# A graph layer on one Trainium2 core: six more message buffers, 128-column first halves, and another spread of the last groups' products

## Chip, cores and metric

The kernel runs on one core of one Trainium2 chip. The metric is device time in microseconds of one execution, shown as the median of several runs. A profile is one further execution, taken by the hardware profiler; its span goes from the first to the last instruction.

## The reference

A pre-normalised relational graph layer on 12,500 nodes of 256 features with 212,500 edges, sorted by destination, each of one of 8 types. There are 200,000 random edges (both directions of 100,000 pairs) and a self edge for every node.

```
h    = relu(layernorm(x))                        # 12500 x 256
hx   = einsum('ni,rio->rno', h, weight)          # 8 x 12500 x 256
msg  = hx[edge_type, src]                        # 212500 x 256
agg  = segment_sum(msg, dst, 12500)
out  = x + agg * 0.5**0.5 + bias + (h @ loop_weight) * 0.5**0.5
```

## The kernel before

It sums first and multiplies afterwards: for each destination node and each type it sums the rows of h, and then multiplies the sums by that type's weight.

**Edges.** The sorted edges lie in units: one partition of an index block holds one unit of 267 consecutive edges (256 in the first block). Self edges of a unit (up to 22) are taken out and added in another way, so that 256 slots, two tiles of 128, hold the rest. Whether all edges were covered is counted, and a general path (line 120) would run behind the rest if not; it does not run here. There are 802 units and 1603 tiles. For a tile, `gather` (line 742) fetches 128 rows of 1 KB into a message tile with one indirect DMA from GpSimd's queue. The rows come from the normalised table h, which the kernel itself writes at the start; before it is complete they come from x and are normalised on chip in batches of four tiles (`batch`, line 1136, and `moments`, line 699). Tile t + AHEAD is gathered in iteration t of the main loop (line 1159). Message tiles are allocated in pairs, MSGS / 2 = 30 pairs; a gather waits until the pair that had its buffer 60 tiles earlier has been multiplied. From the second block on, every tile whose number is 47 modulo 48 is fetched with 128 row DMAs of SP (`load_sources`, line 762) instead, up to t + AHEAD < 1603.

**Sums.** `onehots` (line 779) makes, for four tiles in one VectorE instruction, a matrix with a one where an edge's node and type stand: 176 columns, that is 22 nodes by 8 types from the unit's base node. It is called in every fourth iteration for the tiles from t + LEAD + 2 on, in 2 + LEAD / 4 buffers. `edge_sums` (line 806) multiplies the message tile's two halves of 128 features with it, into one of four PSUM banks per unit. The unit's second multiplied tile holds its first 128 edges; its product covers only `REACH[0][1]` = 13 nodes, 104 columns, except in the last block (tiles from 1536 on), where both cover 22 nodes, 176 columns. In the profile each matmul call is two instructions, so a tile has four. `add_sums` (line 831) adds a unit's bank, one unit behind, to the sums `acc` in SBUF, at an offset from a register; `acc` is a ring of six groups of 128 nodes.

**Groups.** The 12,500 nodes are 98 groups of 128 (the last has 84). `Plan` bounds, from straight lines with a margin, which nodes a unit can touch: `low` and `high`. `plan.last[g]` is the last unit that can touch group g, and after its `add_sums` the group is ready: 18 products (`product`, line 1003, two instructions each: two for h times the loop weight from `self_t`, sixteen for the sums) are put into `queue` with a time from which they may go (`ready`, DELAY = 6 tiles later, less at the end) and one by which they must (`until`). Lines 1207 to 1214 take out as many products per tile as the queue's `until` values demand, after the tile's own matmuls. The products of group g go to the bank `outs[g % 2]`, whose second half holds the bias. After the last one, `last` puts `finish` (line 1021) into a list, to be run REST = 3 tiles later: it adds the bias and the bank to the rows of x and stores them. What is left when the loop ends runs after it (line 1239), lists before products.

**Row buffers.** Tiles of 4 x 128 rows (`rowp`, six buffers) carry, in order of allocation, the 26 pieces of x that are normalised and written to h, and then the rows of x and h that the groups need. When the last piece is normalised (`norms_end`, line 1123, in iteration 28), SP loads bias and weights (`load_weights`, line 1105); six iterations later VectorE copies the bias into the banks and ScalarE scales the weights (`scale_weights`, line 1114).

**Order.** Each engine executes its instructions in the order in which the loop issues them; only waits on semaphores connect engines. GpSimd's queue holds the gathers, SP's all other DMAs. The column tiles (`cols`, three buffers) hold the one-hot positions of a block of 256 tiles; `marks` holds the marks and the diagonal matrix with which `find_types` (line 910) finds, once every four groups, the types of the self edges.

Of the kernel before, what the change touches and what calls it, by code (L numbers as in the profile page):

```python
# [9 lines left out]
F32 = mybir.dt.float32  # L10
BF16 = mybir.dt.bfloat16
# [11 lines left out]
P = 128  # L23
# [4 lines left out]
XG = 4  # L28


EDGES = 267
# [1 line left out]


WIN = 22
REACH = ((0, 13), (0, 22))

GROUP = 128

# [1 line left out]
CLEARED = 3  # L41
RING = GROUP * SLOTS

MSGS = 60
AHEAD = 58

SINGLE = 48
FETCH = 4
# [2 lines left out]


QUAD = 4
LEAD = 8
PAIR = 2
LAG = 1
BANKS = 4
# [1 line left out]

DELAY = 6  # L60
REST = 3

BATCH = 4

# [15 lines left out]
class Plan:  # L80
# [7 lines left out]
    def __init__(self, N, E):  # L88
        U = PAIR * P
        first = P * U  # L90
        self.NU = NU = -(-E // U) if E <= first else P + -(-(E - first) // EDGES)
        self.EU = E - (NU - 1) * U if E <= first else E - first - (NU - P - 1) * EDGES
        self.NT = NU * PAIR - (1 if self.EU <= P else 0)
        self.rate = N / E * EDGES
        s = 6.5 * (E / 4) ** 0.5 + EDGES

        lines = [(U, 0), (EDGES, first - P * EDGES)]
        last = (1.1 * EDGES, 1.1 * (first - P * EDGES) - 0.1 * E - 1.5 * EDGES + s)
        self.low = [(a * N / E, (b - s) * N / E) for a, b in [*lines, last]]
        self.high = [(a * N / E, (b + s) * N / E) for a, b in lines]  # L100
        self.starts = list(range(0, N, GROUP))
        self.ends = self.starts[1:] + [N]
        self.NG = len(self.starts)
        self.last = [
            min([NU - 1, *(int((e + 2 - b) / a) + 1 for a, b in self.low)]) for e in self.ends]
        self.last[-1] = NU - 1
        self.first = [
            max(0, min(int((s - WIN - 2 - b) / a) for a, b in self.high) - 1) if s else 0
            for s in self.starts]

        self.blocks = [
            [k for k in range(1, -(-NU // P))
             if max(a * P * k + b for a, b in self.low) <= e + 2
             and max(a * min(NU - 1, P * k + P - 1) + b for a, b in self.high) + WIN + LASTS + 2 >= s]
            for s, e in zip(self.starts[::XG], self.starts[XG::XG] + [N])]
        self.typed = min([q for q, b in enumerate(self.blocks) if b], default=len(self.blocks))
        assert XG * self.typed >= SLOTS
# [102 lines left out]
def kernel(  # L220
# [11 lines left out]
    nc = tc.nc  # L232
    N, D = x.shape
    E = src.shape[0]
    R = weight.shape[0]
    KC = D // P
    C = R * max(n for _, n in REACH)
    assert KC * R * WIN <= 512
    plan = Plan(N, E)
# [17 lines left out]
    const = ctx.enter_context(tc.tile_pool(name="const", bufs=1))  # L257
    ident = const.tile([P, P], F32, name="ident")
    eps = const.tile([P, 1], F32, name="eps")
    ones = const.tile([P, 1], F32, name="ones")  # L260
    bias_in = const.tile([P, D], F32, name="bias_in")
    w = const.tile([P, KC, R * D], F32, name="w")
    wl = const.tile([P, KC, D], F32, name="wl")
    low = const.tile([P, NB], F32, name="low")
# [17 lines left out]
    with ExitStack() as main:  # L282
# [4 lines left out]
        ep = main.enter_context(tc.tile_pool(name="ep", bufs=1))  # L287
        rowp = main.enter_context(tc.tile_pool(name="rowp", bufs=ROWS))
        idx = main.enter_context(tc.tile_pool(name="idx", bufs=2))
        cols = main.enter_context(tc.tile_pool(name="cols", bufs=3))  # L290
        small = main.enter_context(tc.tile_pool(name="small", bufs=4))
        msgs = main.enter_context(tc.tile_pool(name="msgs", bufs=MSGS // PAIR))
        ohs = main.enter_context(tc.tile_pool(name="ohs", bufs=2 + LEAD // QUAD))
# [2 lines left out]
        marks = main.enter_context(tc.tile_pool(name="marks", bufs=1))  # L296
# [16 lines left out]
        firsts, stops, loops, marked, typed, gidx, col = {}, {}, {}, {}, {}, {}, {}  # L313
# [168 lines left out]
        def columns(b, got):  # L482


            halves = [(slice(i * P, (i + 1) * P), o, n)
                      for i, (o, n) in enumerate(REACH if b < NB - 1 else ((0, WIN), (0, WIN)))]

# [422 lines left out]
        def find_types(q):  # L910

            ptt = pt[:, : XG * (LASTS + 2)].rearrange("p (g k) -> p g k", g=XG)

            def find():
                parts = [(b, m, i) for b, m in marked.pop(q) for i in range(2)]
                for g in range(XG):
                    for b, m, i in parts:
                        nc.tensor.matmul(
                            ptt[:, g, :], m[:, i, g * GROUP : (g + 1) * GROUP], loops[b][:, i, :],
                            start=(b, m, i) == parts[0], stop=(b, m, i) == parts[-1])  # L920

            def kinds_of():
                place_ = small.tile([P, XG], F32, name="place_")
                nc.vector.tensor_scalar(
                    place_, ptt[:, :, LASTS], float(-plan.starts[XG * q]), None, op0=ALU.add)
                nc.vector.tensor_tensor(place_, place_, ptt[:, :, LASTS + 1], op=ALU.add)
                nc.vector.tensor_tensor(place_, node, place_, op=ALU.subtract)
                one = small.tile([P, XG, LASTS], F32, name="one")
                nc.vector.tensor_tensor(
                    one, line[:, :LASTS].unsqueeze(1).to_broadcast([P, XG, LASTS]),  # L930
                    place_.unsqueeze(2).to_broadcast([P, XG, LASTS]), op=ALU.is_equal)
                nc.vector.tensor_tensor(one, one, ptt[:, :, :LASTS], op=ALU.mult)
                kinds = small.tile([P, XG], F32, name="kinds")
                nc.vector.tensor_reduce(kinds, one, AX.X, ALU.add)  # L934
                marked[q] = marks.tile([P, XG * GROUP], BF16, name="diagonal")
                for g in range(XG):
                    nc.scalar.activation(  # L937
                        marked[q][:, g * GROUP : (g + 1) * GROUP], ident, AF.Copy,
                        scale=kinds[:, g : g + 1])

            shared(find, [(2, kinds_of)])

            def spread():
                nc.tensor.matmul(pt, ones_b, marked.pop(q), start=True, stop=True)

            def types_of():
                typed[q] = types.tile([P, XG * GROUP], BF16, name="types")
                nc.scalar.activation(typed[q], pt, AF.Copy)

            shared(spread, [(1, types_of)], lambda: q in marked, wait=2)  # L950

        got = {}
# [104 lines left out]
        with tc.manual_schedule():  # L1057
# [19 lines left out]
            for f in load[1 : 1 + head]:  # L1077
                f()
            for t in range(min(AHEAD, NT)):
                gather(t)  # L1080
# [22 lines left out]
                           for g in range(CLEARED, min(SLOTS, plan.NG))]  # L1103

            def load_weights():
                nc.sync.dma_start(
                    bias_in, bass.AP(tensor=bias.tensor, offset=bias.offset, ap=[[0, P], [1, D]]))
                for c in range(KC):
                    nc.sync.dma_start(
                        w[:, c, :].rearrange("p (r o) -> p r o", r=R),  # L1110
                        weight[:, c * P : (c + 1) * P, :].rearrange("r p o -> p r o"))
                    nc.sync.dma_start(wl[:, c, :], loop_weight[c * P : (c + 1) * P, :])

            def scale_weights():
                for o in outs:
                    i = nc.vector.tensor_copy(o[:, 1, :], bias_in)
                done["bias"] = i.ins.name
                for c in range(KC):
                    nc.scalar.mul(w[:, c, :], w[:, c, :], scale)
                    nc.scalar.mul(wl[:, c, :], wl[:, c, :], loop_scale)  # L1120
                done["weights"] = True
# [37 lines left out]
            for t in range(NT):  # L1159
# [57 lines left out]
                while waiting and (len(waiting) > LAG or t == NT - 1):  # L1217
                    u, ps = waiting.pop(0)
                    add_sums(u, ps)
                    while (next_group < plan.NG and plan.last[next_group] <= u  # L1220
                           and (done["weights"] or (NT <= 400 and done["norm"] == len(pieces)))):
                        g = next_group
                        while background and NT <= 400:
                            step()
                        until = PAIR * (plan.first[g + SLOTS] - 3) - REST if g + SLOTS < plan.NG else NT - 1
                        ready = t + max(0, min(DELAY, NT - 1 - t - 2 * DELAY))
                        until = max(ready, min(until, ready + int(GROUP / plan.rate * PAIR)))
                        if g and g % SLOTS == 0:
                            wrap(g)
                        work = [] if g else group_ahead(0)  # L1230
                        work += group_work(g)
                        if g + 1 < plan.NG:
                            work[-8:-8] = group_ahead(g + 1)
                        for c, f in work:
                            queue.append((ready, until, c, f))
                        next_group += 1
# [36 lines left out]
```

## Time and profile before

| | us |
|---|---|
| median of 3 runs | 2020.34 |
| the runs | 2019.54, 2020.34, 2027.53 |
| profiled execution | 2021.12 |
| its span | 2019.4 |
| PE busy, matmul instructions | 1776.1, 10411 |
| PE's busy time in `edge_sums`, in `product` | 1127.6; 901.5 + 107.8 |
| GpSimd busy | 1497.1 |
| VectorE busy | 1318.5 |
| ScalarE busy | 218.5 |

The granted TensorE clock averages 0.951 of full speed; in the windows it is 0.50 from 50 to 100 us, 0.60 from 100 to 150, and 0.93 to 1.00 after that. Times of an engine in the profile are those of its own instructions; a DMA that GpSimd issues counts there with the time that the issue takes, and the transfer runs on. Matmuls overlap, so that the mean duration of one is longer than the distance between two starts. In groups of instructions the columns are line, engine, operation, what is written and read, count, busy us, mean ns of one, and the idle time before them with what ended it; a releaser is inferred, and where the engine named had long been done it was another. "L758" is the gather's line, L821 the matmul of `edge_sums`, L835 the add of `add_sums`, L1012 the matmul of `product`, L1024 and L1025 the adds of `finish`, L788 the one-hots, L716 the normalising, L736 the write of h.

### The profile page before, as it was taken

What the parts mean: (1) busy time and instruction counts of PE and PEld (TensorE: products, weight loads), DVE (VectorE), ACT (ScalarE), POOL (GpSimd) and SP (SyncE); (2) the same over time, 40 slices, a digit from 0 to 9 for tenths busy, and PEclk for the clock granted to TensorE, in tenths of its full rate; (3) what the DMA queues carried; (4) which work ended last, traced back from release to release, by engine and by line L of the source; (5) the groups of instructions that cost most, each with busy time, mean ns of one, the idle gap of its engine ahead of it and who ended that gap; (6) DMA issues with size and microseconds to landing.
All of it is one profiled execution on the core that took longest, in us unless ns stands there. A gap on an engine that the chain in (4) does not pass through costs nothing.

```text
span 2019.4 us, 36387 instructions
## 1 busy us (share of the span) xinstructions
PE 1776.1 (88%) x10411; PEld 1585.9 (79%) x10411; DVE 1318.5 (65%) x3282; ACT 218.5 (11%) x470; POOL 1497.1 (74%) x1602
## 2 busy tenths in 40 slices
PE   2458999998998898999998998898998898988998
PEld 2357999997888888888777777787787787877886
DVE  7869667687665578656577655578565568665642
ACT  7844110000000000000000000000000000000000
POOL 7757777777777777777777777777777777777773
PEclk8569999998999999999999999999999999999999
DMA  8963443444444444444444444444444444444442
GB/s 296 378 219 100 148 137 106 128 144 122 128 140 120 139 137 119 128 118 139 130 126 139 128 125 134 129 127 140 128 118 139 127 122 129 119 139 122 118 121 70
DMA packets 152577, 281.63 MB, mean 139 GB/s; under 512 B 31149, under 2 KB 101940, under 8 KB 152372
## 3 DMA queue, kind: packets, MB, share of 16 engines
q0 software_dynamic: 75648, 206.67, 34.6%
q1 hardware_dynamic: 76724, 72.61, 11.3%
q8 instruction: 82, 1.34, 0.3%
q14 instruction: 123, 1.01, 0.2%
HBM read 253.55 MB, written 25.60 MB: 138 GB/s over the span
## 4 chain that ended last, share of the span: by engine, by line
PE 36%; DMA 19%; SPq 15%; issue 13%; POOL 8%; DVE 5%; ACT 2%; DVEq 0%; ACTq 0%; POOLq 0%
PE ps L821 19%; PE po L1012 17%; DMA msg<-h,gidx 14%; SPq L770 11%; POOL msg L758 8%; SPq L765 3%; ACT xt L716 1%; DMA h<-xt 1%; DMA hr<-h 1%; DMA msg<-h 1%; DVE e_stats L704 1%; DVE acc L835 1%; DMA w<-in_L_gnn_weight_dram 1%; DVE oh L788 1%; DMA xr<-in_x_dram 1%
## 5 line engine op out<-in xcount | busy, mean ns | idle before, releaser
L758 POOL DMA_INDIRECT msg<-h,gidx x1480 | 1404.0, 949 | 464.9 <-issue 365.4
L821 PE MATMUL ps<-oh,msg 128*128 128x176 f32 (+1 forms) x6412 | 1127.6, 305 | 219.3 <-DMA msg<-h,gidx 88.3
L821 PEld LDWEIGHTS ps<-oh,msg 128*128 128x128 f32 x6412 | 1023.4, 197 | 377.5 <-DMA msg<-h,gidx 175.6
L1012 PE MATMUL po<-w,acc 128*128 128x256 f32 x3136 | 901.5, 390 | 0.7 <-DVE acc L835 0.7
L835 DVE TENSOR_TENSOR acc<-acc,ps 128x352 f32 x802 | 415.4, 518 | 496.2 <-PE ps L821 490.0
L1012 PEld LDWEIGHTS po<-w,acc 128*128 128x128 f32 x3136 | 538.1, 194 | 24.0 <-DVE acc L835 1.3
L788 DVE TENSOR_TENSOR oh<-fixed,cols 128x704 f32<-128x704 f32 x402 | 353.4, 880 | 0.0
L884 DVE SCALAR_TENSOR_TENSOR acc<-types,pt 128x256 f32<-128x256 bf16 (+1 forms) x688 | 249.4, 413 | 84.3 <-PE pt L862 79.3
L867 ACT ACTIVATE self_t<-pt 128x256 f32<-128x256 f32 x98 | 37.5, 383 | 1456.2 <-DVE acc L884 1387.8
L758 POOL DMA_INDIRECT msg<-in_x_dram,gidx x96 | 91.1, 949 | 31.0 <-issue 25.0
L1012 PE MATMUL po<-wl,self_t 128*128 128x256 f32 x392 | 107.8, 399 | 6.5 <-ACT self_t L867 2.6
L1012 PEld LDWEIGHTS po<-wl,self_t 128*128 128x128 f32 x392 | 70.0, 199 | 13.3 <-ACT self_t L867 3.0
L1024 DVE TENSOR_TENSOR xr<-xr,po 128x256 f32<-128x256 f32 x98 | 40.5, 413 | 18.2 <-PE po L1012 16.7
L716 ACT ACTIVATE xt<-xt,n_shift,n_rstd 128x256 f32<-128x256 f32 x98 | 50.9, 588 | 8.9 <-DVE n_shift L713 8.9
L716 ACT ACTIVATE msg<-msg,e_shift,e_rstd 128x256 f32<-128x256 f32 x96 | 49.6, 588 | 12.9 <-DVE e_shift L713 12.9
L1025 DVE TENSOR_TENSOR xr<-xr,po 128x256 f32<-128x256 f32 x98 | 41.2, 421 | 3.4
L937 ACT ACTIVATE diagonal<-ident,kinds 128x128 bf16<-128x128 f32 x88 | 28.1, 390 | 135.2 <-DVE kinds L934 130.7
L862 PE MATMUL pt<-ident,hr 128*128 128x128 f32 x196 | 38.4, 279 | 0.0
L371 DVE TENSOR_SCALAR moves<-fixed 128x267 int32<-128x267 int32 x84 | 36.0, 429 | 1.1
L704 DVE BATCH_NORM_STATS2 n_stats<-xt 128x6 f32<-128x256 f32 x98 | 34.4, 412 | 2.9 <-DMA xt<-in_x_dram 2.1
L372 DVE COPY_PREDICATED fixed<-moves,fixed 128x266 int32<-128x266 int32 (+6 forms) x84 | 33.7, 401 | 2.9
L704 DVE BATCH_NORM_STATS2 e_stats<-msg 128x6 f32<-128x256 f32 x96 | 33.5, 411 | 0.0
(201 smaller groups left out, 321.1 us busy)
## 6 DMA issues: line engine op xcount, KB each, us to landing
msg<-h SPq DMA_DIRECT2D x3456, 1.0 KB
msg<-h,gidx POOLq DMA_INDIRECT x1480
xt<-in_x_dram SPq DMA_DIRECT2D x24, 512.0 KB
h<-xt SPq DMA_DIRECT2D x24, 512.0 KB
xr<-in_x_dram SPq DMA_DIRECT2D x24, 512.0 KB
hr<-h SPq DMA_DIRECT2D x24, 512.0 KB
out_dram<-xr SPq DMA_DIRECT2D x24, 512.0 KB
w<-in_L_gnn_weight_dram SPq DMA_DIRECT2D x2, 1024.0 KB
```

The costliest lines, as they stand in the source:

```text
L704: nc.vector.bn_stats(stats[:n, j, :], rows_[j])
L716: nc.scalar.activation(rows_[j], rows_[j], AF.Relu, bias=shift[:n, j : j + 1], scale=rstd[:n, j : j + 1])
L758: nc.gpsimd.indirect_dma_start(out=msg[t], out_offset=None, in_=table[:, :], in_offset=bass.IndirectOffsetOnAxis(ap=gidx[b][:, at : at + 1 ...
L765: _, vals = nc.values_load_multi_w_load_instructions(single[b][u : u + 1, r0 : r0 + SOURCES], engines=[SP], min_val=0, max_val=(N - 1) * D ...
L770: fetches.insert(0, (0, lambda i=i, v=v: nc.sync.dma_start(msg[t][r0 + i : r0 + i + 1, :].bitcast(U8), h32_bytes[:, bass.ds(v, D * 4)])))
L788: j = nc.vector.tensor_tensor(o[:, k : k + v, :i, :], iota_f.unsqueeze(1).unsqueeze(1).to_broadcast([P, v, i, C]), of.unsqueeze(3).to_broa ...
L821: j = nc.tensor.matmul(ps[:, c, :width], m[:, c * P : (c + 1) * P], o[:, :width], start=(i == 0 and c == 0), stop=(end and c == KC - 1))
L835: i = nc.vector.tensor_tensor(a, a, ps, op=ALU.add)
L884: i = nc.vector.scalar_tensor_tensor(acc[:, :, r, s0 : s0 + n], of, float(r + 1), pst[:, :, :n], op0=ALU.is_equal, op1=ALU.mult)
L1012: i = nc.tensor.matmul(got["out", g][:n], lhs, rhs, start=(r == R and c == 0), stop=(r == R - 1 and c == KC - 1))
L1024: nc.vector.tensor_add(rows_[:n, k, :], rows_[:n, k, :], outs[g % 2][:n, 1, :])
L1025: nc.vector.tensor_add(rows_[:n, k, :], rows_[:n, k, :], got["out", g][:n])
```

## The change

It sets six more message buffers and gathers 64 tiles ahead, widens the first halves' products from 13 to 16 nodes (104 to 128 columns), makes one-hots four tiles ahead in three buffers and no longer eight in four, moves the last of the three lower lines of `Plan`, and sets `until` for the last eight groups (90 to 97) to at most six tiles after `ready`. The bias has no tile of its own any more but a row buffer, the column tiles have two buffers, and the diagonal matrix shares a buffer with the first mark.

```diff
--- before.py
+++ after.py
@@ -33,7 +33,7 @@
 
 
 WIN = 22
-REACH = ((0, 13), (0, 22))
+REACH = ((0, 16), (0, 22))
 
 GROUP = 128
 
@@ -41,8 +41,8 @@
 CLEARED = 3
 RING = GROUP * SLOTS
 
-MSGS = 60
-AHEAD = 58
+MSGS = 66
+AHEAD = 64
 
 SINGLE = 48
 FETCH = 4
@@ -51,7 +51,7 @@
 
 
 QUAD = 4
-LEAD = 8
+LEAD = 4
 PAIR = 2
 LAG = 1
 BANKS = 4
@@ -59,6 +59,7 @@
 
 DELAY = 6
 REST = 3
+SOON = 8
 
 BATCH = 4
 
@@ -95,7 +96,7 @@
         s = 6.5 * (E / 4) ** 0.5 + EDGES
 
         lines = [(U, 0), (EDGES, first - P * EDGES)]
-        last = (1.1 * EDGES, 1.1 * (first - P * EDGES) - 0.1 * E - 1.5 * EDGES + s)
+        last = (1.05 * EDGES, 1.05 * (first - P * EDGES) - 0.05 * E - 0.8 * EDGES + s)
         self.low = [(a * N / E, (b - s) * N / E) for a, b in [*lines, last]]
         self.high = [(a * N / E, (b + s) * N / E) for a, b in lines]
         self.starts = list(range(0, N, GROUP))
@@ -258,7 +259,6 @@
     ident = const.tile([P, P], F32, name="ident")
     eps = const.tile([P, 1], F32, name="eps")
     ones = const.tile([P, 1], F32, name="ones")
-    bias_in = const.tile([P, D], F32, name="bias_in")
     w = const.tile([P, KC, R * D], F32, name="w")
     wl = const.tile([P, KC, D], F32, name="wl")
     low = const.tile([P, NB], F32, name="low")
@@ -287,7 +287,7 @@
         ep = main.enter_context(tc.tile_pool(name="ep", bufs=1))
         rowp = main.enter_context(tc.tile_pool(name="rowp", bufs=ROWS))
         idx = main.enter_context(tc.tile_pool(name="idx", bufs=2))
-        cols = main.enter_context(tc.tile_pool(name="cols", bufs=3))
+        cols = main.enter_context(tc.tile_pool(name="cols", bufs=2))
         small = main.enter_context(tc.tile_pool(name="small", bufs=4))
         msgs = main.enter_context(tc.tile_pool(name="msgs", bufs=MSGS // PAIR))
         ohs = main.enter_context(tc.tile_pool(name="ohs", bufs=2 + LEAD // QUAD))
@@ -932,7 +932,8 @@
                 nc.vector.tensor_tensor(one, one, ptt[:, :, :LASTS], op=ALU.mult)
                 kinds = small.tile([P, XG], F32, name="kinds")
                 nc.vector.tensor_reduce(kinds, one, AX.X, ALU.add)
-                marked[q] = marks.tile([P, XG * GROUP], BF16, name="diagonal")
+                marked[q] = marks.tile(
+                    [P, 2, XG * GROUP], BF16, tag="mark0", name="diagonal")[:, 0, :]
                 for g in range(XG):
                     nc.scalar.activation(
                         marked[q][:, g * GROUP : (g + 1) * GROUP], ident, AF.Copy,
@@ -1103,6 +1104,7 @@
                            for g in range(CLEARED, min(SLOTS, plan.NG))]
 
             def load_weights():
+                bias_in = got["bias"] = rowp.tile([P, XG, D], F32, tag="rows", name="biasr")[:, 0, :]
                 nc.sync.dma_start(
                     bias_in, bass.AP(tensor=bias.tensor, offset=bias.offset, ap=[[0, P], [1, D]]))
                 for c in range(KC):
@@ -1113,7 +1115,7 @@
 
             def scale_weights():
                 for o in outs:
-                    i = nc.vector.tensor_copy(o[:, 1, :], bias_in)
+                    i = nc.vector.tensor_copy(o[:, 1, :], got["bias"])
                 done["bias"] = i.ins.name
                 for c in range(KC):
                     nc.scalar.mul(w[:, c, :], w[:, c, :], scale)
@@ -1225,6 +1227,8 @@
                         until = PAIR * (plan.first[g + SLOTS] - 3) - REST if g + SLOTS < plan.NG else NT - 1
                         ready = t + max(0, min(DELAY, NT - 1 - t - 2 * DELAY))
                         until = max(ready, min(until, ready + int(GROUP / plan.rate * PAIR)))
+                        if g >= plan.NG - SOON:
+                            until = min(until, ready + DELAY)
                         if g and g % SLOTS == 0:
                             wrap(g)
                         work = [] if g else group_ahead(0)
```

## The prediction

> **What bounds the kernel now.** I read the page's table of groups first, then the windows of all engines, then GpSimd's own timeline, then the end of the chain of waits.
>
> ```profile
> L758 POOL DMA_INDIRECT msg<-h,gidx x1480 | 1404.0, 949 | 464.9 <-issue 365.4
> L758 POOL DMA_INDIRECT msg<-in_x_dram,gidx x96 | 91.1, 949 | 31.0 <-issue 25.0
> ```
>
> There are 1576 gathers, 949 ns each, and the idle time before them is nearly all "issue", that is, no wait.
>
> ```profile
> 300.00:400.00 100.00, 100.00 (x639) 94.49 (x639) 69.14 (x148) 5.33 (x14) 75.63 (x81) 1.00 0.40 118
> 1200.00:1300.00 100.00, 90.07 (x523) 75.90 (x521) 56.80 (x121) 3.80 (x10) 75.60 (x81) 1.00 0.44 132
> ```
>
> The columns are length, busy us and instructions of PE, PEld, DVE, ACT and POOL, then clock, DMA share and GB/s. GpSimd issues 80 or 81 gathers per 100 us in both windows, whether PE is full (first line) or a tenth idle (second). One gather starts every 0.949 + 0.30 = 1.25 us; 1576 x 1.25 = 1970 us of the 2019.4 us span. So the gather queue sets the time, and 75.6% "busy" is its full rate. Pairing each tile's gather with its first matmul shows how: tile 202 is multiplied 45 us after its gather starts, tile 706 4.4 us after, and from there to the end 3 to 7 us. PE begins late, is the slower to about 900 us, catches up, and then waits for gathers; being late cost nothing as long as GpSimd was not held. The span is therefore: head (first gather at 4.7 us) + 1576 x 1.25 + what holds GpSimd + what comes after the last gather. Head and number of gathers stay as they are here; the last two terms can change.
>
> What holds GpSimd:
>
> ```profile
> 128.86 0.94 POOL L758 DMA_INDIRECT msg<-h,gidx  x1 [0.30 <-issue]
> 134.98 0.94 POOL L758 DMA_INDIRECT msg<-h,gidx  x1 [5.18 <-ACT e_rstd L708]
> 136.23 0.95 POOL L758 DMA_INDIRECT msg<-h,gidx  x1 [0.30 <-issue]
> 142.96 0.94 POOL L758 DMA_INDIRECT msg<-h,gidx  x1 [5.79 <-issue]
> ...
> 146.17 0.94 POOL L758 DMA_INDIRECT msg<-h,gidx  x1 [1.02 <-ACT e_rstd L708]
> ...
> 188.83 0.94 POOL L758 DMA_INDIRECT msg<-h,gidx  x1 [2.73 <-issue]
> ```
>
> These are the gathers of tiles 100, 102, 104 and 136 (one more, tile 140, is held 0.18 us). The releaser named is not the real one: each starts 0.75 us after the last matmul of the pair 60 tiles before it (tile 41 ends 134.2, tile 43 142.2, tile 77 188.1), so it waits for its message buffer. The holds sum to 4.87 + 5.48 + 0.72 + 2.42 + 0.18 = 13.7 us. PE is late there because normalising, then the weight load (chain: "DMA w" 14.87 us from 113.46), hold ACT and so the messages. After 194 us no gather waits for a buffer again; the distance grows to 68 us.
>
> The end:
>
> ```profile
> 1995.56 4.32 PE po L1012 x20
> 1999.87 0.60 PE ps L821 x4
> 2000.47 3.88 PE po L1012 x18
> 2004.36 0.61 PE ps L821 x4
> 2004.97 0.02 issue
> 2004.99 0.52 DVE acc L835
> 2005.51 0.34 DVE xr L1024
> 2005.86 0.02 issue
> 2005.88 0.43 DVE xr L1025
> 2006.31 0.14 issue
> 2006.44 7.99 PE po L1012 x36
> ```
>
> The last gather starts at 1992.75, and 26.65 us follow: PE has a backlog of products of groups 95 and 96 among the last tiles, waits 1.47 us, then does group 97's 36 matmuls (7.99 us); 4.97 us of adds and output end it.
>
> **The change, part by part.**
>
> *66 buffers, 58 to 64 tiles ahead.* The count of gathers stays 1576 (the 27 tiles fetched by SP stay the same 27, since 1535 + 64 < 1603). The same matmul ends now release gathers six tiles later, and those are due 6 x 1.25 = 7.5 us later. Running the row's pace against the same releases: tile 108 is held 2.8 us (due 140.1, freed 142.9), 110 0.72, 142 2.64, 146 0.18; tile 146 starts at 194.0, where tile 140 does now. Gain 7.5 us. It would be 14 if PE's releases did not matter, and each buffer is worth 1.25.
>
> *What that brings with it.* The gathers from h begin six tiles later, at quads: 100 tiles come from x, not 96. That is one more batch of norms: on DVE 4 x 0.411 + 4 x 0.152 + 0.173 + 0.167 = 2.6 us, on ACT 0.29 + 4 x 0.588 = 2.6 us, near 206 us, where DVE is full to 210 and partly idle after. Behind it on DVE wait the adds that free PE's banks for tiles 92 to 98. Tile 97 frees the gather of tile 162, which has 1.0 us to spare, so this costs 0 to 1.6 us; I take 0.3, since DVE idles from 211 and PE alone sets the pace there. SP's row fetches are issued six tiles (7.5 us) earlier against use; PE's 48.7 us of waits for them lie where PE is behind anyway: 0.
>
> *First halves 128 columns.* By form, the 128x104 matmuls take 282 ns, the 128x176 ones 327, and the transposes, which stream 128 columns against a 128x128 weight, 279. In a full stretch (305 to 322 us) starts are 112 ns apart at 104 columns, 109 at 128 (transposes) and 149 at 176: at 104 the 128-wide weight load already sets the spacing. Cost 0; upper bound by the slope between 104 and 176 columns, 45 / 72 x 24 = 15 ns x 3072 = 46 us of PE work, under the 10 us in 100 that PE idles from 950 on, and 1.2 us in the 20 first halves between tiles 41 and 81. The Trainium skill ("TensorE: Matmul & The Clock Gate", section Back-to-back issue gap) has a gap that grows with the streamed columns, N/2.4 + 2.5 ns, beside a weight load that grows with the weight's columns; by the first alone 24 columns are 10 ns, an estimate of 0.8 us off the gain through those 20 halves, by the second nothing. The 112 and 109 ns speak for the second.
>
> *One-hots four tiles ahead, not eight.* The 0.88 us one-hot of a quad is still ahead of the bank-freeing add that PE's same tile needs (made at iteration 2v-6 or 2v-8 for tile 2v, the add at 2v-5), in one in-order queue. So PE's wait stays the add. 0; at best one 0.88 us op less before the first tiles.
>
> *Bias in a row buffer.* On SP the bias load now waits for the h write of row piece 20, issued at 93.28 and landed 6.5 us later, 12 us before the bias is issued (111.95); weights and the first groups' rows queue behind it. 0; were it piece 25's write (about 111.6), 5 us later weights. Two column buffers, the diagonal in a mark's tile: each reuse follows work in the same queue or a transpose done four groups before. 0.
>
> *Later line and SOON.* I worked the queue of products through the plan's formulas. Groups 84 to 96 become ready 1 to 3 units earlier, and groups 90 to 95 put 18 products into six tiles (4, 3, 3, 3, 3, 2). Group 95 lies in tiles 1589 to 1594 (now 1590 to 1600), group 96 in 1598 to 1601 as 5, 5, 5, 3 (now 9 in 1600, 9 in 1601). A tile is 0.60 us of PE, a product two matmuls, 0.43. Now PE last waits for a gather at tile 1593 (landed 4.2 us after its start; 2.75 is usual); 10 tiles and 30 products later is 2004.75, and the trace has 2004.97. Changed, it last waits at tile 1589: 1976.50 + 2.75 + 14 x 0.60 + 36 x 0.4325 = 2003.2. Only 1.7 us, 1.1 of it that landing: the same work stands behind nearly the same last wait. The 1.47 us wait is group 97's first product, on the same output bank as 95, whose finish is queued three tiles after its last product: tile 1603, after the loop. It becomes 1597, and the last add (0.52) hides under group 97's four self matmuls (0.86): 1.4 us. Tail gain 3.1; from 1.5 (a late landing at 1589) to 4.
>
> **Sum.** 7.5 - 0.3 + 3.1 = 10.3 us off the profiled execution's 2021.12 (span 2019.4 and 1.7 around it): 2010.8. That execution is 0.8 over the median of 2020.34, so against the median it is 9.5 us or 0.47%, just inside the 0.5% (10.1 us, 2010.2) that I take as what a measurement tells from no change.
>
> **Rivals.**
>
> *More at the start.* If the one-hot less (0.88) reaches tile 41 through the norms and the new batch costs nothing: 8.4 + 3.1, 2009.6; with tail at 4, 2008.7. For: from 93 to 112 us the chain goes through DVE and ACT. Against: DVE idles 10 us before 130.8, waiting for the weights, which swallows it unless the weights too come earlier.
>
> *The buffers bring little.* If PE's releases move as much as the buffers give (batch, wider halves at the half clock of 50 to 145 us), only the tail is left: 2018.0. For: the held stretch is set by PE, DVE and ACT, none of which gets faster. Against: they wait for nothing that gathers 100 to 146 bring.
>
> *Slower: the weights come late.* If the bias load waits in SP's queue for a row buffer that frees late, the weight loads behind it, ACT's scaling, the norms queued behind that, and tiles 40 on all shift, and GpSimd is held one for one. From 10.3 us of delay the kernel is slower; at 15 us it takes 2025.8. Against: the h writes are done 12 us before.
>
> *It doesn't do what it says.* If the last groups' ready times did not move, the tail would stay and 2013.9 come out; the formulas exclude it nearly.
>
> **How the numbers follow.** My forecast 0.62 (own range 2009 to 2013, 4 in 10 of it under 2010.2), more at the start 0.18, buffers that bring little 0.12, slower 0.06, tail unmoved 0.02. Faster: 0.25 + 0.18 = 0.43; within: 0.37 + 0.12 + 0.02 - 0.01 = 0.50; slower 0.07 with a hundredth for what I did not see. The range 2007.5 to 2016 leaves out the third and fourth cases.
>
> **What would show it.** GpSimd's holds before 200 us: four, near 140, 145, 186 and 194, summing to 6 to 8 us, and the last gather's start near 1985.5. Form lines: 128x128 matmuls of L821 at 279 to 285 ns; over 297 the wider halves cost. Bias issued at 112 and the second weight scaling at 128.4. At the end no DVE xr between tile 1602 and group 97, and 23.5 us after the last gather's start. Wrong would be a gather pace other than 1.25 us (6.5 ns more eats all), holds past 210 us, or PE idle before group 97.

## The result

| | before | after |
|---|---|---|
| median, us | 2020.34 | 2010.41 |
| runs, us | 2018.90 to 2027.53 (5) | 2008.48 to 2011.17 (5) |
| profiled execution, us | 2021.12 | 2008.48 |
| its span, us | 2019.4 | 2006.8 |

The ratio, taken over all runs, is 0.9943, with a 95% interval of 0.9925 to 0.9962; before's run of 2027.53 counts in it. The medians lie 9.9 us apart, a ratio of 0.9951; 10.3 us were predicted off the profiled execution. After's profiled execution is the shortest of its five, so the spans differ by 12.6 us, 2.7 more than the medians.

Groups of after's page (line, engine, operation, count; busy us, mean ns; idle before):

```profile
L758 POOL DMA_INDIRECT msg<-h,gidx x1476 | 1400.1, 949 | 454.1 <-issue 362.3
L758 POOL DMA_INDIRECT msg<-in_x_dram,gidx x100 | 94.9, 949 | 32.4 <-issue 27.1
```

Again 1576 gathers of 949 ns; four have moved from h to x.

The windows of all engines, after (length; busy us and instructions of PE, PEld, DVE, ACT, POOL; clock, DMA share, GB/s):

```profile
300.00:400.00 100.00, 100.00 (x639) 94.47 (x638) 69.33 (x147) 5.32 (x14) 75.64 (x80) 1.00 0.43 126
1200.00:1300.00 100.00, 88.34 (x520) 76.19 (x519) 57.12 (x122) 3.79 (x10) 75.61 (x80) 1.00 0.44 127
```

GpSimd's rate is what it was, 75.6% "busy", with PE full or a tenth idle. What has shrunk are the holds. GpSimd's timeline, after (start us, duration, what; in brackets the idle time before, of which 0.30 is usual):

```profile
141.48 0.94 POOL L758 DMA_INDIRECT msg<-h,gidx  x1 [1.48 <-issue]
...
144.25 0.94 POOL L758 DMA_INDIRECT msg<-h,gidx  x1 [0.57 <-issue]
...
146.97 0.94 POOL L758 DMA_INDIRECT msg<-h,gidx  x1 [0.30 <-ACT msg L716]
149.22 0.95 POOL L758 DMA_INDIRECT msg<-h,gidx  x1 [1.31 <-PE pt L862]
...
185.85 0.94 POOL L758 DMA_INDIRECT msg<-h,gidx  x1 [0.50 <-issue]
...
192.39 0.95 POOL L758 DMA_INDIRECT msg<-h,gidx  x1 [1.85 <-issue]
```

These are the gathers of tiles 108, 110, 112, 113, 142 and 146. No idle time is over 2 us, where before had 5.18, 5.79 and 2.73. (In the 146.97 line the hold of 0.22 us is in the longer issue ahead of it, not in its bracket.)

The chain that ended last, after (start us, duration, what):

```profile
1967.06 2.77 DMA msg<-h,gidx
1969.83 0.04 issue
1969.87 0.86 PE ps L821 x4
1970.74 1.73 PE po L1013 x8
...
1989.39 2.16 PE po L1013 x10
1991.55 0.60 PE ps L821 x4
1992.14 1.29 PE po L1013 x6
1993.44 0.60 PE ps L821 x4
1994.04 7.78 PE po L1013 x36
2001.82 0.02 issue
2001.84 0.43 DVE xr L1025
```

PE waits for a gather for the last time at tile 1589, with an ordinary landing of 2.77 us; from there it runs through, and group 97's 36 matmuls follow the last tile at once. The adds of `finish` between the last tile and group 97, at 2005.5 and 2005.9 before, are gone from the chain.

The span taken apart by pairing the nth gather with the nth gathered tile. "Holds" adds up, for gathers that start between 20 and 215 us, what the distance from one start to the next has over 1.25 us, where that is more than 0.1 us; "later" is the same after 215 us.

| execution | span | first gather | holds | later | start to start, median ns | after the last gather's start |
|---|---|---|---|---|---|---|
| before | 2019.4 | 4.72 | 13.9 | 3.9 | 1251 | 26.66 |
| after | 2006.8 | 4.94 | 4.5 | 3.4 | 1251 | 23.49 |
| change | -12.6 | +0.2 | -9.4 | -0.5 | 0 | -3.2 |

The columns add up to 12.9 us, 0.3 more than the spans differ by; that is 0.2 ns a gather the other way.

### The profile page after: what moved, and what is told of

Same layout as the page of the kernel before. It is cut to its first block, busy times and chain, and to the rows that moved or that the text cites. A ratio compares the mean times of both kernels' runs of the same rounds, so it can differ in the third digit from the quotient of the medians.

```text
span 2006.8 us, 36408 instructions
## 1 busy us (share of the span) xinstructions
PE 1766.0 (88%) x10411; PEld 1587.0 (79%) x10411; DVE 1317.5 (66%) x3292; ACT 220.9 (11%) x475; POOL 1497.0 (75%) x1602
## 4 chain that ended last, share of the span: by engine, by line
PE 29%; SPq 27%; DMA 16%; issue 14%; POOL 6%; DVE 5%; ACT 2%; DVEq 0%; ACTq 0%; POOLq 0%
SPq L770 20%; PE ps L821 15%; PE po L1013 14%; DMA msg<-h,gidx 9%; SPq L765 6%; POOL msg L758 6%; DMA hr<-h 2%; DMA xr<-in_x_dram 2%; DMA h<-xt 1%; ACT xt L716 1%; DVE acc L835 1%; DVE e_stats L704 1%; DVE oh L788 1%; DMA w<-in_L_gnn_weight_dram 1%; DMA xt<-in_x_dram 1%
## 5 line engine op out<-in xcount | busy, mean ns | idle before, releaser
L821 PE MATMUL ps<-oh,msg 128*128 128x176 f32 (+1 forms) x6412 | 1131.5, 307 | 216.7 <-DMA msg<-h,gidx 78.5
L1013 PE MATMUL po<-w,acc 128*128 128x256 f32 x3136 | 880.6, 384 | 1.5 <-DVE acc L835 1.5
L788 DVE TENSOR_TENSOR oh<-fixed,cols 128x704 f32<-128x704 f32 x402 | 353.1, 879 | 0.0
L1013 PEld LDWEIGHTS po<-wl,self_t 128*128 128x128 f32 x392 | 70.3, 200 | 10.3 <-ACT self_t L867 3.0
```

The lines of the kernel that those rows point to most:

```text
L788: j = nc.vector.tensor_tensor(o[:, k : k + v, :i, :], iota_f.unsqueeze(1).unsqueeze(1).to_broadcast([P, v, i, C]), of.unsqueeze(3).to_broa ...
L821: j = nc.tensor.matmul(ps[:, c, :width], m[:, c * P : (c + 1) * P], o[:, :width], start=(i == 0 and c == 0), stop=(end and c == KC - 1))
L1013: i = nc.tensor.matmul(got["out", g][:n], lhs, rhs, start=(r == R and c == 0), stop=(r == R - 1 and c == KC - 1))
```

## The experiments

Each kernel is the changed one with the edit shown. Ratios are to the kernel before, run beside it on the same chip, and are taken over all runs, so that they need not be the ratio of the medians.

**Only the buffers undone.**

```diff
-MSGS = 66
-AHEAD = 64
+MSGS = 60
+AHEAD = 58
```

> The changed kernel with 60 buffers and 58 tiles ahead again, everything else as changed. Buffer theory (a gather waits for the matmul 60 or 66 tiles before it, each buffer is worth one gather start of 1.25 us): holds of GpSimd before 215 us grow by about 7.5 us over the changed kernel's 4.5, to 11 to 12; the end after the last gather's start stays at 23.5; time about 7 us over the changed kernel, near 2017.5. Rival, the start is quicker for another reason (one-hots four ahead, the bias in a row buffer): holds stay at 4 to 6 us and the time stays near 2010.5. If tile 41's matmuls end near 133 us here too, and not 134.2, the 1.3 us by which they came earlier do not come from the buffers.

2022.1 us (median of 11), ratio 0.9987 (0.9978 to 0.9996). GpSimd's timeline of this kernel:

```profile
129.18 0.94 POOL L758 DMA_INDIRECT msg<-h,gidx  x1 [0.30 <-issue]
135.09 0.95 POOL L758 DMA_INDIRECT msg<-h,gidx  x1 [4.97 <-ACT e_rstd L708]
```

The long holds are back: 4.67 us at tile 100 (this line), 5.48 at 102, and 13.5 in all (11 to 12 were expected), while 23.77 us follow the last gather's start, without a wait before group 97. So the rest of the change, tail included, is worth 0.13%, 2.6 us (0.8 to 4.4), and the buffers the rest: 0.9987 - 0.9943 = 0.44%, 8.9 us, or by the intervals 5 to 13. There is a closer comparison: the kernel with 104 columns (below), run beside this one on the same chip, which has the 66 buffers and differs from after in the halves alone, had a median of 2014.68, 7.4 us less than this one. Tile 41's matmuls ended at 134.3 us here, as in before (134.2), and not at 133; the sign by which after's 1.3 us would have come from something other than the buffers did not appear. Its profiled span is 14.8 us over after's, more than that; the gathers explain the difference:

```profile
L758 POOL DMA_INDIRECT msg<-h,gidx x1480 | 1408.8, 952 | 464.9 <-issue 360.5 <-PE ps L821 63.2 <-DMA msg<-h,gidx 15.9
```

In this execution each issue takes 3 ns more, 4.7 us over 1576; with 9.0 of holds, 0.9 later, 0.3 after the last gather, and 0.1 off at the first, it is 14.8.

**The tail undone, whole and by halves.**

```diff
-SOON = 8
+SOON = 0
-        last = (1.05 * EDGES, 1.05 * (first - P * EDGES) - 0.05 * E - 0.8 * EDGES + s)
+        last = (1.1 * EDGES, 1.1 * (first - P * EDGES) - 0.1 * E - 1.5 * EDGES + s)
```

> The changed kernel with the old lower line and without the earlier limit for the last eight groups. Tail theory: 26 to 26.7 us from the last gather's start to the end and not 23.5, a wait of about 1.5 us of PE on the adds of the group before the last, and nothing else moves: holds before 215 us near 4.5, time 2 to 3 us over the changed kernel, near 2013. Rival, the spread is what brings the gain: 8 to 10 us over, near 2019. Rival, the tail is hidden: no change.

2016.12 us (5 runs), ratio 0.9958 (0.9944 to 0.9971). Its interval overlaps that of after, so the times alone don't separate them; the chain of waits does:

```profile
1972.44 3.94 DMA msg<-h,gidx
1976.42 0.86 PE ps L821 x4
...
1990.53 0.60 PE ps L821 x4
1991.12 3.88 PE po L1013 x18
1995.01 0.61 PE ps L821 x4
1995.64 0.52 DVE acc L835
1996.16 0.34 DVE xr L1025
1996.53 0.43 DVE xr L1026
1997.10 7.99 PE po L1013 x36
```

That is the end of the kernel before, with 66 buffers: a late landing (3.94 us, tile 1593), 18 matmuls in one tile, and PE idle from 1995.62 to 1997.10, 1.48 us, until `finish` has read the bank. 26.40 us follow the last gather's start; with before's 26.66 and after's 23.49 the tail is worth 2.9 to 3.2.

Then only SOON undone, with the new line:

> The changed kernel without the earlier limit for the last eight groups (SOON 0), with the new lower line. By the queue worked through the plan's formulas group 95's last product then lies in tile 1598 and its finish in 1601, still inside the loop, and the products behind PE's last wait for a gather are as many. Theory: 23.5 us from the last gather's start to the end, no wait before group 97, as in the changed kernel. Rival, the limit is what shortens the end: 26 us or more and the 1.5 us wait is back.

2010.11 us (3 runs), ratio 0.9951 (0.9935 to 0.9968); 23.85 us after the last gather's start, no wait before group 97. And only the line undone, with SOON = 8:

> The changed kernel with the old lower line, the limit for the last eight groups kept. Worked through the formulas group 95 ends in tile 1595, its finish in 1598; group 96 stays at 10 and 8 products in tiles 1600 and 1601. Theory: the wait before group 97 is gone and 23.5 to 24.5 us follow the last gather's start. Rival, both edits are needed: 25 us or more.

2009.39 us (2 runs), ratio 0.9942 (0.9920 to 0.9963); 24.50 us, no wait. Of the 3.2 us between before and after the line alone gives 2.8 and SOON alone 2.2, so the two are not gains that add up: they are two ways to nearly the same end. Each alone removes the wait; these are single executions.

**First halves of 104 columns again, and of 176.**

```diff
-REACH = ((0, 16), (0, 22))
+REACH = ((0, 13), (0, 22))
```

> The changed kernel with first halves of 13 nodes, 104 columns. Theory that the weight load sets the spacing: in full stretches a 104-column matmul starts 112 ns after the one before, as a 128-column one does, and the time stays within 1 us of the changed kernel, since the gathers set it. Rival, streamed columns count: spacing 20 ns shorter (3072 x 20 ns = 61 us of PE work), PE catches up with the gathers some 300 tiles earlier, and if PE's lateness at the start matters the holds before 215 us shrink by up to 1.5 us.

2014.68 us (5 runs), ratio 0.9949 (0.9935 to 0.9962), as after. Here tiles 41 and 43 ended at 134.2 and 142.2 us, to the tenth as before, which makes this execution the test of the predicted holds:

```profile
142.93 0.95 POOL L758 DMA_INDIRECT msg<-h,gidx  x1 [3.11 <-issue]
```

Tile 108 is held 2.80 us (3.11 less 0.30) until 142.93; predicted were 2.8 and 142.9. The sum is 6.1, predicted 6.3, but that closeness is luck: tile 142 was held 1.25 us and not 2.64, tile 110 0.37 and not 0.72, and tile 113, for which nothing was predicted, 1.1.

```diff
-REACH = ((0, 16), (0, 22))
+REACH = ((0, 22), (0, 22))
```

> The changed kernel with first halves of 22 nodes, 176 columns like the second ones: 3072 matmuls start 149 ns after the one before and not 112, 114 us more PE work over the whole. Gather theory: GpSimd's pace and the end stay, PE is only later to catch up (after tile 1200, not near 800), and at the start it costs at most the 20 first halves between tiles 41 and 81, 3 us more of holds: 0 to 4 us over the changed kernel in the same session. Rival, PE's work sets the time: 30 us or more over it.

2010.05 us (4 runs), ratio 0.9943 (0.9926 to 0.9961). Page and window of this kernel:

```profile
L821 PE MATMUL ps<-oh,msg 128*128 128x176 f32 x6412 | 1225.7, 322 | 152.6 <-DVE acc L835 44.3
```

```profile
1200.00:1300.00 100.00, 93.66 (x525) 86.31 (x524) 57.11 (x121) 3.80 (x10) 75.58 (x81) 0.97 0.42 124
```

`edge_sums` has 94 us more of busy time than after (1225.7 against 1131.5), or, by the spacing of starts in full stretches, 3072 x (149 - 112) ns = 114 us, and the time doesn't move. GpSimd's rate is still 75.6%. PE catches up with the gathers later (tile 874 is still multiplied 13.5 us after its gather, after's 4.4; before the last tiles this distance is over 10 us up to tile 900, in after up to 773), though earlier than tile 1200, which was expected. It does catch up, and the time is that of after.

**Two buffers more**, paid for with one of the two type buffers.

```diff
-MSGS = 66
-AHEAD = 64
+MSGS = 68
+AHEAD = 66
-        types = main.enter_context(tc.tile_pool(name="types", bufs=2))
+        types = main.enter_context(tc.tile_pool(name="types", bufs=1))
```

> Two more buffers, 68 and 66 ahead; the types tile has one buffer and not two to make room. Buffer theory: another 2 x 1.25 us less hold as far as holds are left (4.5 us before 215 us), so 2 to 2.5 us under the changed kernel, near 2008. Rival, the holds left are not of the buffers (releases later by as much): no change. If the one types buffer delays ACT or DVE, tiles 77 to 101 end later than in the changed kernel and the holds at 186 to 192 us grow.

2013.7 us (5 runs), ratio 0.9938 (0.9924 to 0.9951): not to be told from after. Its profiled execution has the same 4.5 us of holds, though the weights came 2.5 us later than in after's (second scaling at 129.49, after 127.02; tile 43 ended at 143.4, after 140.7). A hold that two buffers save was taken back by the weights, so this run neither shows nor excludes 2.5 us. The one types buffer may delay tile 101, which ended 89.3 us after the second scaling (in after 87.3), but the holds there are only 0.28 and 0.16 us.

**Fewer gathers.** The count of gathers, which the change leaves alone, is what the theory says the time hangs on. Here every 36th tile is fetched by rows and not every 48th, in turn from SP's and ACT's queues, and 1568 gathers are left.

```diff
+ACT = mybir.EngineType.Activation
-SINGLE = 48
+SINGLE = 36
-                single[b][u : u + 1, r0 : r0 + SOURCES], engines=[SP],
+                single[b][u : u + 1, r0 : r0 + SOURCES], engines=[SP, ACT],
-                fetches.insert(0, (0, lambda i=i, v=v: nc.sync.dma_start(
+                fetches.insert(0, (0, lambda i=i, v=v: (nc.sync, nc.scalar)[i % 2].dma_start(
```

> The changed kernel with every 36th tile and not every 48th fetched by single-row DMAs, their rows taken in turn from SP's and ScalarE's queue: 35 tiles so fetched and not 27, 1568 gathers and not 1576. Gather theory: 8 x 1.25 = 10 us less, near 2000 where the changed kernel takes 2010, since ScalarE is 89% idle. Rival, ScalarE's copies that PE waits for (self rows, type tiles) queue behind the row DMAs, or the rows land late: PE waits longer for them than the 55 us in all that it waits for rows in the changed kernel, and the gain is under 3 us or a loss.

1999.71 us (1998.89 to 2000.54, 4 runs), ratio 0.9893 (0.9876 to 0.9911): faster than both kernels. 8 gathers fewer are 8 x 1.25 = 10 us. Three kernels with 1576 gathers that ran beside it on the same chip (the line only, SOON only, 176 columns) had medians of 2009.4 to 2010.1, 10 us more; the ratios, 0.9943 - 0.9893 = 0.50%, say the same. PE's waits no longer name the fetched rows (55.5 us in after), so the rival is out. The last gather starts at 1974.14, 9.1 us before after's, with 24.14 behind it.

```profile
1200.00:1300.00 100.00, 90.55 (x526) 77.90 (x527) 57.10 (x122) 3.79 (x10) 75.61 (x81) 0.98 0.43 127
```

The rate of gathers is untouched; there are only fewer of them.

**One-hots made as late as can be, and still fewer gathers.** The next four runs ran on two other chips, where the kernel before itself took 2593 us (2581 to 2604) and 2571 us (2558 to 2579), so they are read against that.

```diff
-LEAD = 4
+LEAD = 0
```

> The changed kernel with one-hots made in the iteration just before their first tile's pair (LEAD 0) and not four tiles ahead. In VectorE's queue the one-hots of tile 2v then come after the add that frees its bank, and are the later of the two things that PE waits for. Order theory (at eight and four ahead the add is the later one, so the step from eight to four is free): this step is not free; PE waits about 0.9 us more per quad where VectorE sets the pace (150 to 205 us), tile 81 ends 3 us or more after the second scaling of the weights plus 64 us, which is what the changed kernel has, and holds grow by 2 to 8 us; after 300 us nothing changes. Rival, the lead doesn't matter at all: tile 81 ends 63 to 66 us after the second scaling starts.

2592.89 us (8 runs), ratio 0.9998 (0.9964 to 1.0031). A group of this kernel:

```profile
L821 PE MATMUL ps<-oh,msg 128*128 128x176 f32 (+1 forms) x6412 | 1177.5, 315 | 457.7 <-DMA msg<-h 185.4 <-DVE oh L788 88.7 <-issue 75.5
```

PE now waits 88.7 us for one-hots (L788), a releaser that the same groups of before and after do not name: at LEAD 4 the one-hot is still ahead of the add, and at 0 it no longer is. The sign named beforehand came: tile 81 ended 67.7 us after the second scaling, in after 64.6 and in the kernels with every 28th tile on these two chips 65.8 and 65.1. What that would cost at 2010 us was not measured, because here something else set the time: "DMA msg<-h", the rows that SP fetches. The time from a fetched tile's first row DMA to its last, and when PE multiplies it, worked out from the traces of three kernels:

| execution | tile | rows issued, from and for, us | multiplied, us | after the last row | since the tile before, start to start |
|---|---|---|---|---|---|
| after | 575 | 680, 56.2 | 738 | 1.9 | 11.7 |
| after | 671 | 797, 55.7 | 854 | 1.8 | 6.6 |
| after | 911 | 1081, 51.8 | 1142 | 8.9 | 1.7 |
| LEAD 0 | 575 | 931, 73.6 | 1006 | 1.6 | 13.3 |
| LEAD 0 | 671 | 1084, 74.0 | 1159 | 1.5 | 12.2 |
| LEAD 0 | 911 | 1466, 71.7 | 1539 | 1.5 | 9.9 |
| every 36th | 575 | 655, 40.0 | 726 | 31.0 | 1.0 |

In after, 128 rows keep SP 51 to 57 us (65 and 67 for two late tiles); with what SP does between them it begins such a tile every 57.3 us, and the 47 gathers between two of them take GpSimd 47 x 1.25 = 58.75. So SP's row queue is just fast enough, and up to tile 815 PE does wait for it, while it still has time to lose. On this chip the rows take 68 to 82 us. The rows of one fetched tile follow those of the other within a few us, from tile 335 on PE multiplies each such tile 0 to 3 us after its last row was issued, and from tile 479 to 1295 it takes 1275 us for 816 tiles, 75.0 us for 48. The gathers are far ahead (tile 874 is multiplied 111 us after its gather). So here SP's rows set the time, not the gathers, and LEAD could hardly show in it.

```diff
-SINGLE = 48
-FETCH = 4
+SINGLE = 28
+FETCH = 6
```

with the two queues of the kernel with every 36th tile; 1558 gathers. First on the chip at 2593 us, with every 24th tile (SINGLE = 24, 1549 gathers) beside it:

> As with every 36th tile fetched by rows from SP's and ScalarE's queues, but every 28th, with six row DMAs per tile at most and not four: 45 tiles by rows, 1558 gathers. Gather theory: 18 x 1.25 = 22 us under the changed kernel, near 1988. Rival, rows land late (SP and ScalarE each issue 64 rows per 34 us, some 26 us of it): PE's waits for rows grow past its spare time and the gain is under 15 us.

> The same with every 24th tile: 54 tiles by rows, 1549 gathers. Gather theory: 27 x 1.25 = 34 us under the changed kernel, near 1976, since PE needs about 1.01 us per tile (0.60 and 0.45 for the two tiles of a unit, 18 products of 0.43 per 16.4 tiles) against 1.21 between gathers. Rival, ScalarE and SP have 29 us for 26 us of row issues and their other DMAs and copies: rows land late, and the time is over 1985.

2686.7 us (4 runs), ratio 1.0342 (1.0289 to 1.0395), and 2919.55 us (4 runs), ratio 1.1235 (1.1181 to 1.1289). Then the first of them on the other chip:

> The changed kernel with the rows of every 28th fetched tile by hardware queues (SP's and ACT's in turn) rather than by a GpSimd gather, so that some 1558 gathers are left rather than 1576; the same program as e14_act_rows28, which ran in a session where the kernel before itself took 2593 us. Theory that the gathers' issue on GpSimd sets the time (1.25 us each): where the kernel before is near 2020, 18 gathers fewer are 22 us off the changed kernel's 2010, near 1988, a ratio near 0.984, below e10's 0.9893. Rival, that the hardware queues' row fetches have become what PE and GpSimd wait for at this density, as e14 showed: not under 2000, a ratio of 0.989 or more, with GpSimd held in the middle of the run. If the kernel before is again near 2590 the run tells nothing on the theory.

2666.68 us (4 runs), ratio 1.0372 (1.0327 to 1.0417). A window of this last run, and the timeline of ScalarE and its DMA queue (ACTq) in it (start us, duration, what, count):

```profile
1200.00:1300.00 100.00, 77.17 (x418) 68.27 (x418) 45.70 (x99) 3.02 (x8) 60.48 (x64) 0.93 0.36 102
```

```profile
1210.40 20.18 ACTq L771 DMA_DIRECT2D msg<-h  x31
1230.68 0.38 ACT L868 ACTIVATE self_t<-pt 128x256 f32<-128x256 f32 x1 [19.77 <-DMA msg<-h]
1232.20 24.83 ACTq L771 DMA_DIRECT2D msg<-h  x31
1256.38 0.38 ACT L868 ACTIVATE self_t<-pt 128x256 f32<-128x256 f32 x1 [25.31 <-issue]
```

64 gathers in 100 us, where after has 80. The rows are not late for PE here: it multiplies a fetched tile 29 to 49 us after its last row was issued. But ScalarE's queue holds nothing but row DMAs, 0.65 us each, and the copy `self_t` that a group needs comes when the 31 rows ahead of it are out. 64 rows a tile are 42 us, and 28 tiles would be gathered in 34, so the queue is never empty. PE's waits name it:

```profile
PE pt L919 <- ACT self_t L868: 230.2, 18, 17.9
```

(us in all, times, longest). Then PE is late, GpSimd runs a whole ring of buffers ahead (tile 874 is multiplied 101 us after its gather, in after 4.4) and is held for them, and the gathers' pace no longer matters. The expectation from the count of gathers failed on both chips. Whether it would hold beside a kernel before of 2020 us stays open; in the kernel with every 36th tile a row in ScalarE's queue took 0.51 to 0.73 us too, as a mean of a tile, so 64 of them (33 to 47 us) would hardly fit into 34 us there either. How every 36th tile fares on such a chip was not tried.

## Why the prediction was right

**The bound.** The gather queue sets the time. Some 100 us of PE work more cost nothing, 8 gathers fewer gave 10 us, and the rate of 75.6% stood in every execution at 2000 to 2020 us that was looked at. The prediction had passed over SP's row queue, a near second with 57.3 us of 58.75, with "where PE is behind anyway": true here, while with LEAD 0 on a slower chip the rows were the bound. Its reading that from tile 706 on a tile is multiplied 3 to 7 us after its gather is a little narrow: the trace of before has 2.7 to 8.4 us, and up to 11.4 in the last tiles. The argument doesn't hang on it.

**Buffers, 7.5 us.** Undoing them alone cost 7.4 us against the 104-column kernel run beside it and 8.9 by the ratios, and the holds went from 13.9 to between 3.7 and 6.6 us in the executions with 66 buffers. The mechanism was right: with tiles 41 and 43 ending as before, tile 108 was held the 2.80 us that were worked out. The later holds were smaller than worked out. The size moves with the weights' landing. In after the second scaling began at 127.02 us and tile 41 ended at 132.9, in before at 128.36 and 134.2. So after's profiled holds were 4.5 us, not 6.3 and not the 6 to 8 named as a sign, and its last gather started at 1983.29, not 1985.5. In the five kernels whose start is the same as after's, after among them, that scaling began between 126.2 and 127.8, so it varies by more than this from one execution to the next; but with 60 buffers it was 128.36 and 128.44, and with 66 and 104 columns 128.33. Whether after's 1.3 us are such a variation or come from the change is open, and with it the rival "more at the start": its 2009.6 us and the forecast's 2010.8 lie on either side of the median of 2010.41. One hold was not foreseen: tile 113, 1.0 to 1.3 us in every 66-buffer kernel looked at, 1.8 with 68, and none with 60. Its cause was not found.

**The new batch, 0.3 us.** Nothing: tile 162 is not held in after.

**Wider halves, 0.** By form, in before and then in after:

```profile
L821 PE MATMUL ps<-oh,msg 128*128 128x104 f32 x3072 | 487.4, 282 | 132.7 <-DMA msg<-h 48.7 <-DVE acc L835 46.8 <-DMA msg<-h,gidx 35.7
```

```profile
L821 PE MATMUL ps<-oh,msg 128*128 128x128 f32 x3072 | 503.7, 287 | 141.3 <-DMA msg<-h 55.5 <-DVE acc L835 45.1 <-DMA msg<-h,gidx 35.7
```

282 to 287 ns, where 279 to 285 were said and 297 would have meant a cost. The prediction's reading that starts are 112 ns apart at 104 columns misses one start in four. Of the four matmuls of a first half, in a full stretch (300 to 400 us), the second starts 89 ns after the first at 104 columns and 109 at 128; the other spacings, to the first of what follows included, are 111 to 112 ns at both widths, and at 176 columns all are 149. So the wider halves do cost PE 20 ns each, 768 x 20 ns = 15 us over the whole and about 0.4 us in the 20 halves between tiles 41 and 81, and the term was put at nothing by a reading that was not quite right. The time doesn't show it, as PE has the time to spare: with 104 columns the distance from gather to matmul is over 10 us up to tile 692, with 128 up to 773. The Trainium skill ("TensorE: Matmul & The Clock Gate", section Back-to-back issue gap) gives the formula that the prediction used as the gap of an isolated matmul, and says that in a stream of weight loads and matmuls both set the spacing. The traces agree that more than the columns counts, since three spacings in four stay as they are; the one that moves does so by 20 ns, not by the 10 of the formula. At 176 columns all four cost PE, and even that did not reach the time.

**One-hots, bias, smaller pools, 0.** SP issued the bias at 112.36 us, 112 was said (111.95 before), so it waits for no row buffer that frees late, and the rival with weights that come late is out. The second scaling was said at 128.4 and came at 127.02, as told above. That half the lead costs nothing rests on the traces of after, where no one-hot is among the releasers that PE's groups name; LEAD 0 shows what too short a lead looks like: there they are named, and tile 81 ended 2 to 3 us later after the scaling.

**The tail, 3.1 us.** 26.66 to 23.49, 3.2, and 23.5 was said. Both halves of the term can be seen: the last wait is at tile 1589 with an ordinary landing, and the 1.47 us before group 97 are gone and come back, as 1.48, when line and SOON are undone. From that landing to group 97 the working gives 23.97 us (14 x 0.60 + 36 x 0.4325); the chain has 24.17 (1969.87 to 1994.04).

**The rest of it.** Terms measured 7.4 to 9.4 (buffers), 0 (batch, tile 162) and 2.9 to 3.2 (tail), which is 10.3 to 12.6 against 10.3; the medians show 9.9. Executions differ in the weights' landing and in the gathers' 3 ns (last section), and either moves the time by more than the 0.4 us between prediction and median. That the two lie so close is in part luck. That the buffers and the tail bring the gain, and about how much each, is not.

## What to carry to other kernels

Where one in-order queue issues at its full rate from end to end, its share of busy time can be 75% and it is still the bound: take the span as head, count x pace, holds, and what follows the last issue, and cost every edit by which of the four it changes. Work on an engine that is late at the start and catches up later is free until it no longer catches up; work that is taken out of the queue counts in full. Whoever takes work out of it by giving it to another queue must compare that queue's time per piece with its due date, and look at what else stands in that queue: 36 to 48 us of rows in 44 us gave a gain, with 17 to 33 us to spare before their use; some 42 in 34, measured on the two slower chips alone, gave a loss.

## What the runs showed that was not expected

In the ten executions at 2000 to 2020 us the gather's issue has one of two durations, nearly from start to end: a median of 946 ns, mean 948.5 to 949.4 (before, after, and the kernels with the old tail, 104 columns, SOON only, and every 36th tile by rows), or a median of 949, mean 951.7 to 952.1 (60 buffers, 68 buffers, the line only, 176 columns). The start-to-start median goes with it, 1251 or 1254. VectorE's one-hots (879 to 880 ns) do not change in step, but the bias was issued at 113.3 to 113.6 us in the executions with the longer issue and at 112.0 to 112.9 in the others. 3 ns x 1576 is 4.7 us, about half of what the change brought, so spans of two single executions can mislead by that much. A median of few runs may too: the profiled execution is the shortest of its kernel's runs with the old tail and with 104 columns, where the issue is the short one, and the longest with the line only and with 176 columns, where it is the long one; with 60 and with 68 buffers it lies in between. What sets the two durations stayed open.

On the two chips with 2571 and 2593 us the gather itself kept its pace (a median of 1251 to 1252 ns start to start). Slower were the loads at the start (from 50 to 100 us 129 to 135 GB/s were moved, in after 381) and the row DMAs (68 to 82 us for 128 with LEAD 0, in after mostly 51 to 57), at a granted clock of 0.83 to 0.89, in after 0.952. A held gather also starts later there: 0.75 us after the last matmul of its buffer in before, by a median of some 5 us in the last run above; this was not followed up. Why these chips differed then is not known; a kernel whose second queue is used to 57.3 of 58.75 us has little margin for one.
